# Two graph attention layers on one core: the scheduler's ring is booked in order of issue with nine slots, the seam's factors take a scalar operand, entry 1's mask moves to ScalarE, and strips run in longer blocks

## The chip, the cores and the metric

The kernel runs on one core of one Trainium2 chip. The metric is the device time of one execution in microseconds. Engines are named as in the profile: PE is TensorE's matmuls, PEld its weight loads, DVE is VectorE, ACT is ScalarE, POOL is GpSimd, SP is SyncE, which here issues the DMAs.

## The reference, cut to what matters

There are eight entries of 2048 nodes with 256 channels, and one adjacency matrix for all. Each entry goes through two layers, each followed by a residual sum and a layer norm.

```
# layer 0: eight heads of 32 channels
x_proj = einsum('bnd,hdf->bhnf', x, W)
e = leaky_relu(e_src[..., :, None] + e_dst[..., None, :], 0.2)
e = e + softplus(beta_tilde) * log(adj + 1e-6)
attn = softmax(where(adj > 0, e, -big))
x = layernorm(x + (attn @ x_proj, heads side by side) @ W_out.T)
# layer 1: one head of 256 channels
e = leaky_relu((x @ W1) @ (x @ W2).T, 0.2)
attention = softmax(where(adj > 0, e, -1e12))
x = layernorm(x + relu(attention @ (x @ W3)))
```

All values are float32.

## The kernel before

**Layer 0** takes two heads at a time (`HP = 2`, four pairs) and half of the rows (`rh`, 1024 of them). That is a unit, and there are eight units per entry. A unit has 16 tiles `s` of 128 partitions x 2 heads x 1024, one for each 128 columns of the adjacency (`jt`). A "strip" is PE's work on such a tile: `val` (the tile times the projected features) and, for some tiles, `den` (the tile times the denominators' weights), eight matmul instructions of 32 columns each, four side by side. From entry 2 on, tiles 11 to 15 of a unit are "direct": DVE makes the two heads' halves from the loaded mask `mt` (line 926), and PE adds up their denominators. Tiles 0 to 10 are "chain" tiles: ACT scales `mt` into the tile (line 399), DVE multiplies (line 926), and POOL adds the tile to the running `sums` (line 934), which PE takes in a last `close` strip. At a unit's end its heads are copied out (`evicted`), divided, and for the second pair of four heads multiplied on POOL (line 491).

**Layer 1** goes over 16 blocks of 128 rows per entry. For each, PE makes the scores `e` (line 1140), ACT copies them into one wide tile `p` (line 1146), DVE takes the mask `pen` off and finds the maximum (line 1185), POOL negates it (line 1186), ACT takes the exponential (line 1191), PE transposes `p` (`T`, line 1214), ACT copies that (line 1219), and PE multiplies with the values (`acc`, line 1233). ACT and DVE then finish the row block: `relu`, `z` (line 1255, which frees the PSUM bank of `acc`), statistics, norm, store.

**The seam** stands between an entry's two layers. PE multiplies the heads by `W_out` (`y`, line 1031), DVE adds the input (line 1035), takes statistics (line 1045), ACT makes the inverse deviation (lines 1051 and 1052), DVE the factor mean times inverse deviation (line 1057), ACT applies both (line 1064), and PE transposes (`tr`, line 1076) and makes the values (`h`, line 1090). Four groups of four row blocks pass through this.

**Order of the work.** Layer 0 of the first entry and the projections of all entries are in an order written out by hand. From then on a small scheduler in the kernel's Python (`Sched`) lays out all engines' instructions, each engine's in a fixed order: it keeps a clock for each engine and each task's assumed time (`busy`) and sets, step by step, the task that can start first. Layer 0 of the next entry (strips) is laid between layer 1 and the seam of the present one ("full" work). In what follows, entry 1 of the scheduled part means layer 1 of the first entry with layer 0 of the second beside it. Buffers are modelled by `Slots`, one list per ring; `Hold` is one use of a buffer that ends with its last reader. The actual buffer is handed out by the tile framework when the kernel is built, from a ring of nine with the tag "s" (`ring_tile`), which is used by the strips' tiles, by the wide tile `p` for all of an entry's layer 1, and by the second `ht` (the upper four heads), which later holds the seam's results.

PE chooses in `choose_pe` between the next full task and the next strip. The lag is the goal (strips in proportion to full work done, plus a lead) less the strips eaten. In a block of strips PE goes on while the lag is over `LOW`; from full work it turns to strips when the lag is over `HIGH` at an easy place and over `STRICT` within an iteration. It takes a strip as well when the full task isn't ready.

```
if f[0] > now + 0.35 or lag > (LOW if self.kind == "strip" else HIGH if easy else STRICT):
    return v[0], v[1], 0
return f[0], "full", f[1]
...
S.goal = lambda w: NP * 2 * NT * (w + 33.0) / span
```

In entry 1 the adjacency rows come in as integers, and the mask `pen` is made from them in two halves, the first on ACT (line 1168) and the second on DVE (line 1171); it is stored, and later entries load it.

Of the kernel before, what the change touches and what calls it, by code (L numbers as in the profile page):

```python
# [18 lines left out]
P = 128  # L19
# [8 lines left out]
def kernel(  # L28
# [38 lines left out]

    J2 = NT // 2
    DIRECT = [[range(NT)] * NP] + [[(11, 12, 13, 14, 15)] * NP] * (B - 1)
    SLOTS = 7  # L70

    const = ctx.enter_context(tc.tile_pool(name="const", bufs=1))
    dram = ctx.enter_context(tc.tile_pool(name="dram", bufs=1, space=DRAM))
# [19 lines left out]
    def ring_tile(name, shape=(P, N)):  # L93


        return wide.tile(list(shape), F32, tag="s", name=name, bufs=9)
# [414 lines left out]
    TURN = {False: 0.0, True: 0.14, ("T", "acc"): 0.11, ("acc", "T"): 0.05, ("acc", "e"): 0.08, ("e", "acc"): 0.085, ("T", "e"): 0.04,  # L511
            ("e", "T"): 0.03, ("e", "val"): 0.12, ("T", "val"): 0.13, ("acc", "val"): 0.08, ("val", "e"): 0.19, ("tr", "h3"): 0.1}
    WINDOW = 8
    LOW, HIGH, STRICT = -1.0, 1.5, 4.0
    NOW = [0.0]
    BACK = 2

# [6 lines left out]
    class Slots:  # L524
# [4 lines left out]
            self.free = [(0.0, tags[i] if tags else i) for i in range(n)]  # L529

        def at(self, n=0):
            return sorted(self.free)[n][0] if len(self.free) > n else None

        def take(self):
            got = min(self.free)
            self.free.remove(got)
            return got[1]

        def give(self, end, tag):
            self.free.append((end, tag))  # L540
# [21 lines left out]
    class Only:  # L562
# [8 lines left out]
        def take(self):  # L571
            self.slots.free.remove(next(f for f in self.slots.free if f[1] == self.tag))
            return self.tag

        def give(self, end, tag):
            self.slots.give(end, tag)
# [222 lines left out]
    S = Sched()  # L799
    bank = Banks(["m0", "m1", "den"])  # L800
    ring, mts, pts_s, hts, rows_s = (Slots(n, None, name) for n, name in ((SLOTS, "ring"), (4, "mt"), (4, "pts"), (4, "ht"), (4, "rows")))
    v_s, c_s, pen_s, xs_s = (Slots(n, None, name) for n, name in ((2, "v"), (0, "c"), (1, "pen"), (2, "xs")))

    def pe(where, name, busy, emit, deps=(), hold=None, reader=None, easy=True, seam=False):
# [50 lines left out]
    def unit(b, hp, rh, vs, vhold):  # L855
# [28 lines left out]
        prev_add = {}  # L884
        for jt in range(NT):
            chain = jt in u.chain
            slot = Hold(ring, 0)
            mt = Hold(mts, 2)
            ring_next = {"slot": slot}

# [3 lines left out]
            mload = S.add("mt", 0.35, load, takes=[mt], late=4.0)  # L894

            def begin(jt=jt):
                u.s[jt] = ring_tile("s", (P, HP, HALF))

            readers = 1 if jt in u.direct else 0
# [77 lines left out]
        if hp == 0 and rh == 0:  # L977
            hold = Hold(hts, 1)
            E.first_hold = hold
            u.evicted = S.add("evict", 0.5, u.copy_values, [u.vals[NT - 1]], takes=[hold])  # L980
        else:
            n = 4 if hp == 0 else 2
            deps = [u.vals[NT - 1]]
            frees = []
            if hp == 0:
                frees = [E.first_hold]
                deps.append(entries[b - 1].last_tr)
            if hp == HP and rh == 0:
                deps.append(entries[b - 1].last_tr)
            u.evicted = S.add("evict", 0.55 * n, u.copy_values, deps, frees=frees)  # L990
        dn = Hold(hts, 1)

        def dn_copy():
# [11 lines left out]
    def seam(b):  # L1005
# [9 lines left out]
        for g in range(NB):  # L1015
            xh, xn = Hold(hts, 2), Hold(xs_s, 2)

            def load(g=g):
                gat.xs[g] = chunk.tile([P, IG, D], F32, tag="ht", name="xg", bufs=4)
                nc.sync.dma_start(gat.xs[g], x[b].rearrange("(t p) d -> p t d", p=P)[:, ts(g, IG), :])  # L1020
            xl = S.add("x", 0.4, load, [E.start] if b else [], takes=[xh, xn], late=4.5)
            ys, st = [], {}
            deps = [E.mult[0, g // 2], E.mult[1, g // 2]]
            if old:
                deps.append(old.lastT)

            def y(t, k, g=g):
                yt = t.rearrange("p (t c) -> p t c", t=2)
                for i in range(2):
                    for kc in range(KC):  # L1030
                        nc.tensor.matmul(yt[:, i, :], gat.ht[kc][:, ts(g * IG + 2 * k + i, P)], wot[:, kc, :],  # L1031
                                         start=(kc == 0), stop=(kc == KC - 1))
            for k in range(2):
                def add(t, k=k, g=g):
                    nc.vector.tensor_add(gat.x1(2 * g + k), t.rearrange("p (t c) -> p t c", t=2), gat.xs[g][:, ts(k, 2), :])
                ys.append(pe("full", "y", 1.83, lambda t, k=k, y=y: y(t, k), deps, Hold(bank, 1), ("sum", 0.62, add, [xl]), seam=True))
            for k in range(2):
                ys[k].reader.deps += ys
                ys[k].reader.frees += [xh, xn]
            stats = []  # L1040
            for k in range(2):
                def stat(k=k, g=g):
                    if k == 0:
                        state["st", g] = small.tile([P, IG // 2, nc.vector.BN_STATS_DIM], F32, name="st4", bufs=2)
                    nc.vector.bn_stats(state["st", g][:, k, :], gat.x1(2 * g + k).rearrange("p t c -> p c t"))
                stats.append(S.add("stats", 0.65, stat, [ys[k].reader]))

            def lnexp(g=g):
                state["mv", g] = mv = state["st", g].rearrange("p a (t c) -> p (a t) c", t=2)
                state["f", g] = f = small.tile([P, 2, IG], F32, name="f4", bufs=2)  # L1050
                nc.scalar.activation(f[:, 0, :], mv[:, :, 2], AF.Ln, bias=eps_ln, scale=1.0 / D)
                nc.scalar.activation(f[:, 0, :], f[:, 0, :], AF.Exp, scale=-0.5)
            ln = S.add("ends", 0.52, lnexp, stats)

            def factor(g=g):
                f, mv = state["f", g], state["mv", g]
                nc.vector.scalar_tensor_tensor(f[:, 1, :], mv[:, :, 1], -1.0, f[:, 0, :], ALU.mult, ALU.mult)  # L1057
            fac = S.add("tinys", 0.1, factor, [ln])
            for k in range(2):
                def end(k=k, g=g):  # L1060
                    z, f = gat.x1(2 * g + k), state["f", g]
                    for i in range(2):
                        row = z[:, i, :]
                        nc.scalar.activation(row, row, AF.Identity, bias=f[:, 1, 2 * k + i:2 * k + i + 1],
                                             scale=f[:, 0, 2 * k + i:2 * k + i + 1])
                r = S.add("ends", 1.05, end, [fac])
                x1_ready[2 * g + k] = r

                def store(k=k, g=g):
                    nc.sync.dma_start(x1_d[b].rearrange("(t p) d -> p t d", p=P)[:, ts(2 * g + k, 2), :], gat.x1(2 * g + k))  # L1070
                E.done[2 * g + k] = S.add("out", 0.4, store, [r], late=3.0)
        for j in range(NT // 2):
            def tr(t, j=j):
                for kc in range(KC):
# [6 lines left out]
                nc.scalar.copy(gat.x1t[:, :, ts(j, 2 * P)], t.rearrange("p (k i) -> p k i", k=KC))  # L1081
            deps = [x1_ready[j], old.lastT if old else None]
            t = pe("full", "tr", 0.46, tr, deps, Hold(bank, 1), ("copy", 0.5, x1c, [old.lastE] if old else []), seam=True)
            trs.append(t)
            E.x1c[j] = t.reader

# [16 lines left out]
    def layer1(b):  # L1103
# [25 lines left out]
            h1[g] = (box, hold, out)  # L1129

        pbox = {}

        def scores(it, c):
            g = it // IG
            box, hold, qs = h1[g]
            r = R[it]

            def mm(t):
                for kc in range(KC):
                    nc.tensor.matmul(t, box["h"][:, kc, ts(it % IG, P)], gat.x1t[:, kc, ts(c, BK)],  # L1140
                                     start=(kc == 0), stop=(kc == KC - 1))

            def pre(t):
                if it == 0 and c == 0:
                    pbox["p"] = ring_tile("p")
                nc.scalar.activation(pbox["p"][:, ts(c, BK)], t, AF.Prelu, alpha=ALPHA)  # L1146
            deps = [qs[0].reader, qs[1].reader, E.x1c[2 * c], E.x1c[2 * c + 1]]
            if it == 0 and b > 0:
                deps.append(entries[b - 1].lastT)
            t = pe("full", "e", 1.74, mm, deps, Hold(bank, 1), ("copy", 0.5, pre, [R[it - 1]["T"][c]] if it else []), easy=(it == 0), seam=(it == 0))  # L1150
            t.frees = [hold]
            r["e"].append(t)

        def soft(it):
# [3 lines left out]
            if b == 0:  # L1158
# [5 lines left out]
                eh = [Hold(hts, 1), Hold(hts, 1)]  # L1164
                ld = S.add("row", 0.8, load, takes=[pen_hold] + eh, late=5.0)

                def half0():
                    nc.scalar.activation(r["pen"][:, ts(0, HALF)], r["edges"][0], AF.Relu, bias=no_edge, scale=-NO_EDGE)

                def half1():  # L1170
                    nc.vector.tensor_scalar(r["pen"][:, ts(1, HALF)], r["edges"][1], 0.0, NO_EDGE, ALU.is_le, ALU.mult)
                m0 = S.add("norm", 1.05, half0, [ld], frees=[eh[0]])
                m1 = S.add("stats", 1.15, half1, [ld], frees=[eh[1]], lock=True)
                S.add("out", 0.4, lambda: nc.sync.dma_start(pen_d[ts(it, P), :], r["pen"]), [m0, m1], late=3.0)
                pen = [m0, m1]
            else:
                def load():
                    r["pen"] = wide_tile("pen", "pen", 1, BF16)
# [28 lines left out]
        def turn(it, c):  # L1207
# [11 lines left out]
                nc.scalar.copy(pt, t)  # L1219
            t = pe("full", "T", 0.46, tr, [r["exp"]], Hold(bank, 1), ("copy", 0.5, cp, []), easy=(c < 1))  # L1220
            t.reader.takes = [hold]
            r["T"].append(t)

        def acc(it, h):
# [90 lines left out]
    for a in range(HP):  # L1315
        u.makes[NT - 1, a].after = lambda a=a: bank.give(u.makes[NT - 1, a].end, f"c{a}")
    span = 303.0
    S.goal = lambda w: NP * 2 * NT * (w + 33.0) / span
    S.run()
# [1 line left out]
_INS = ['x', 'adj', 'L0_gnn_W', 'L0_gnn_a_src', 'L0_gnn_a_dst', 'L0_gnn_beta_tilde', 'L0_gnn_W_out',  # L1321
# [27 lines left out]
```

## Time and profile before

| | |
|---|---|
| time, median of 3 runs | 4218.2 us (4212.86 to 4220.96) |
| the profiled execution | 4212.3 us, span 4210.1 us |
| PE, DVE, ACT, POOL busy | 4016.7, 3190.9, 2914.5, 2746.0 us |
| mean granted TensorE clock | 0.987 |
| DMA | 843.63 MB, mean 200 GB/s |

A busy share is an average over stages. PE's time counts a matmul from its start to a modelled end, and matmuls overlap, so PE's idle time is read from starts. In rows by line the columns are: line, engine, operation, tile written and tiles read, shapes, count, then busy us and mean ns, then the engine's idle time before them and what ended it. In rows of one tile the three numbers behind the count are the shortest, median and longest duration in ns. In a timeline they are start and length in us, then engine and line, and in brackets the idle time before and its releaser.

### The profile page before, as it was taken

The numbers are of one execution on the slowest core, as the hardware profiler recorded it, in microseconds if no ns is written. First come the engines' busy times: TensorE is split into PE (matmuls) and PEld (weight loads), VectorE is DVE, ScalarE is ACT, GpSimd is POOL, SyncE is SP. The second block draws the span as 40 slices with busy tenths as digits, with TensorE's granted clock in tenths as the row PEclk, the third lists the DMA queues.
The fourth block names the chain that finished last, engine by engine and source line by source line (L and its number), as shares of the span: only waits on it lengthen the run. The fifth ranks groups of instructions, "written<-read, shape, count | busy, mean of one in ns | idle before, by whom it ended". The sixth has DMA issues, their size and how long they took to land.

```text
span 4210.1 us, 60355 instructions
## 1 busy us (share of the span) xinstructions
PE 4016.7 (95%) x22704; PEld 2151.3 (51%) x22704; DVE 3190.9 (76%) x3263; ACT 2914.5 (69%) x4148; POOL 2746.0 (65%) x1318
## 2 busy tenths in 40 slices
PE   7899799998999999999999999999999999999999
PEld 5444344444555554454555545555555555555666
DVE  7888688877888888777888878787888887775222
ACT  6522467776787778776777778777777777776554
POOL 0000278877788886877878878888788886885000
PEclk9999899999999999999999999999999999999999
DMA  7888767666566666555666565656665665554111
GB/s 263 281 279 291 246 215 241 227 218 218 190 215 203 203 196 208 202 197 194 204 203 196 199 215 201 206 188 213 210 205 197 201 229 195 193 189 136 62 47 41
DMA packets 346437, 843.63 MB, mean 200 GB/s; under 512 B 49696, under 2 KB 166432, under 8 KB 346144
## 3 DMA queue, kind: packets, MB, share of 16 engines
q1 hardware_dynamic: 346144, 839.77, 59.6%
q8 instruction: 178, 2.92, 0.3%
q14 instruction: 115, 0.94, 0.1%
HBM read 763.76 MB, written 75.37 MB: 199 GB/s over the span
## 4 chain that ended last, share of the span: by engine, by line
PE 63%; ACT 8%; DVE 7%; POOL 5%; DMA 3%; issue 3%; SPq 0%; DVEq 0%; ACTq 0%; POOLq 0%
PE e L1140 19%; PE acc L1233 17%; PE val L445 13%; POOL sums L934 5%; PE den L445 4%; DVE s L926 4%; PE T L1214 4%; ACT s L399 4%; PE h L1090 3%; PE h L1116 2%; ACT p L1146 1%; DMA mt<-mt_d 1%; DVE f L1057 1%; DVE p L1185 1%; PE y L1031 1%
## 5 line engine op out<-in xcount | busy, mean ns | idle before, releaser
L934 POOL TENSOR_TENSOR sums<-sums,s 128x1024 f32<-128x1024 f32 x1008 | 2365.7, 2385 | 29.3 <-DVE s L926 27.3
L926 DVE SCALAR_TENSOR_TENSOR s<-c,re,s 128x1024 f32<-128x1024 f32 x1232 | 1512.9, 1274 | 304.6 <-ACT s L399 252.2
L399 ACT ACTIVATE s<-mt,re 128x1024 f32<-128x1024 f32 x1232 | 1353.9, 1146 | 127.5 <-DMA mt<-mt_d 58.8
L445 PE MATMUL val<-s,v 128*32 128x512 f32 x8192 | 1026.1, 599 | 41.4 <-DVE s L413 13.7
L1140 PE MATMUL e<-x1t,h 128*128 128x512 f32 x2048 | 988.9, 607 | 45.4 <-ACT p L1146 33.7
L1233 PE MATMUL acc<-h,pts 128*128 128x256 f32 x4096 | 927.5, 382 | 0.7 <-ACT pts L1219 0.7
L1233 PEld LDWEIGHTS acc<-h,pts 128*128 128x128 f32 x4096 | 768.4, 190 | 226.5 <-issue 106.2
L926 DVE SCALAR_TENSOR_TENSOR s<-c,re,mt 128x1024 f32<-128x1024 f32 x560 | 682.5, 1274 | 93.0 <-POOL sums L934 86.6
L1140 PEld LDWEIGHTS e<-x1t,h 128*128 128x128 f32 x2048 | 352.9, 191 | 402.0 <-issue 269.9
L445 PEld LDWEIGHTS val<-s,v 128*32 128x32 f32 x8192 | 236.2, 109 | 608.2 <-issue 478.0
L1185 DVE CUSTOM_DVE_ANT_0 p<-p,pen 128x2048 f32<-128x2048 f32 x128 | 320.2, 2502 | 229.8 <-ACT p L1146 228.7
L1146 ACT ACTIVATE p<-e 128x512 f32<-128x512 f32 x512 | 304.3, 594 | 202.5 <-PE e L1140 198.0
L445 PE MATMUL den<-s,re 128*32 128x512 f32 x3264 | 438.7, 593 | 0.0
L1186 POOL TENSOR_SCALAR neg<-neg 128x1 f32<-128x1 f32 x128 | 26.7, 208 | 627.8 <-DVE neg L1185 627.8
L934 POOL TENSOR_TENSOR sums<-s 128x1024 f32<-128x1024 f32 x112 | 266.9, 2402 | 254.3 <-DVE s L926 218.3
L1191 ACT ACTIVATE p<-p,neg 128x2048 f32<-128x2048 f32 x128 | 256.1, 2001 | 246.6 <-POOL neg L1186 246.3
L1214 PEld LDWEIGHTS T<-ident,p 128*128 128x128 f32 x2048 | 251.0, 141 | 275.5 <-issue 174.6
L413 DVE SCALAR_TENSOR_TENSOR s<-c_in,re,mt 128x1024 f32<-128x1024 f32 x256 | 310.4, 1277 | 49.1 <-DMA mt<-mt_d 36.7
L1214 PE MATMUL T<-ident,p 128*128 128x128 f32 x2048 | 309.8, 275 | 21.7 <-ACT p L1191 19.1
L1219 ACT COPY pts<-T 128x512 f32<-128x512 f32 x512 | 297.0, 583 | 28.0 <-PE T L1214 27.2
L286 POOL PARTITION_ALL_REDUCE top<-top x8 | 6.6, 820 | 431.0 <-DVE top L285 415.1
L445 PEld LDWEIGHTS den<-s,re 128*32 128x32 f32 x3264 | 109.3, 110 | 243.3 <-issue 240.7
(100 smaller groups left out, 2538.1 us busy)
## 6 DMA issues: line engine op xcount, KB each, us to landing
mt<-mt_d SPq DMA_DIRECT2D x992, 512.0 KB
c_in<-c_d SPq DMA_DIRECT2D x64, 1024.0 KB
pen<-pen_d SPq DMA_DIRECT2D x112, 512.0 KB
xg<-in_x_dram SPq DMA_DIRECT2D x60, 512.0 KB
adj_t<-in_adj_dram SPq DMA_DIRECT2D x16, 1024.0 KB
mt_d<-mt SPq DMA_DIRECT2D x32, 512.0 KB
rb<-rec_d SPq DMA_DIRECT2D x128, 128.0 KB
adj_r<-in_adj_dram SPq DMA_DIRECT2D x32, 512.0 KB
```

Of the source, the lines that this page charges most:

```text
L399: nc.scalar.activation(self.s[jt][:, a], self.mt[jt], AF.Copy, scale=self.gat.re[:, 1, jt, h:h + 1])
L413: nc.vector.scalar_tensor_tensor(s[:, a], self.c[a], self.gat.re[:, 0, jt, h:h + 1], m, ALU.max, ALU.mult)
L445: nc.tensor.matmul(dst[ts(q, DH), :], weights[q % 2], s[:, q % 2, ts(q // 2, BK)], start=start, stop=stop)
L926: nc.vector.scalar_tensor_tensor(u.s[jt][:, a], u.c[a], gat.re[:, 0, jt, h:h + 1], m, ALU.max, ALU.mult)
L934: nc.gpsimd.tensor_tensor(u.sums[:, a], of[:, a], u.s[jt][:, a], ALU.add)
L1140: nc.tensor.matmul(t, box["h"][:, kc, ts(it % IG, P)], gat.x1t[:, kc, ts(c, BK)], start=(kc == 0), stop=(kc == KC - 1))
L1146: nc.scalar.activation(pbox["p"][:, ts(c, BK)], t, AF.Prelu, alpha=ALPHA)
L1185: nc.vector.tensor_tensor_reduce(p, p, r["pen"], 1.0, -FMAX, ALU.subtract, ALU.max, neg)
L1191: nc.scalar.activation(p, p, AF.Exp, bias=r["neg"], accum_out=den)
L1214: nc.tensor.transpose(t[:, ts(k, P)], pbox["p"][:, ts(c * IG + k, P)], ident)
L1219: nc.scalar.copy(pt, t)
L1233: nc.tensor.matmul(r["acc"], r["pts"][g][:, ts(k, P)], gat.h3[:, j, :], start=(j == 0), stop=(j == NT - 1))
```

## The change

It has five parts.

1. `Slots` gives out the buffer that was given back first in order of issue, where it was the one with the earliest free time. This holds for all rings.
2. The ring is booked with nine slots instead of seven. What was left out before (the wide tile `p` and the second `ht`) is now booked by `Hold`s of its own: one per entry for `p`, from the first score copy to the last transpose, and one for the heads, from the copy to the seam's stores and transposes. The class `Spare` lets strips' tiles take a slot only if enough are left for these two (`keep` counts how many are reserved).
3. The seam's factor is made by four `tensor_scalar` instructions over one element each instead of one `scalar_tensor_tensor` over four, and is booked with 0.35 instead of 0.1 us.
4. In entry 1 both halves of the mask are made on ACT.
5. `LOW`, `HIGH` and `STRICT` are -2, 4 and 8 instead of -1, 1.5 and 4; the lead is 28 instead of 33.

```
-    SLOTS = 7
+    SLOTS = 9
...
-    LOW, HIGH, STRICT = -1.0, 1.5, 4.0
+    LOW, HIGH, STRICT = -2.0, 4.0, 8.0
...
         def at(self, n=0):
-            return sorted(self.free)[n][0] if len(self.free) > n else None
+            return self.free[n][0] if len(self.free) > n else None
 
         def take(self):
-            got = min(self.free)
-            self.free.remove(got)
-            return got[1]
+            return self.free.pop(0)[1]
...
+    class Spare:
+        def __init__(self, slots):
+            self.slots, self.keep, self.name = slots, 0, "spare"
+
+        def at(self, n=0):
+            return None if self.slots.at(n + self.keep) is None else self.slots.at(n)
+
+        def take(self):
+            return self.slots.take()
 
         def give(self, end, tag):
             self.slots.give(end, tag)
...
+    spare = Spare(ring)
+    spare.keep = 1
+    heads_hold = [Hold(ring, 2 * NB + NT // 2)]
+    heads_hold[0].take()
...
-            slot = Hold(ring, 0)
+            slot = Hold(spare, 0)
...
             def begin(jt=jt):
+                if jt == 0 and hp == HP and rh == 0:
+                    spare.keep += 1
                 u.s[jt] = ring_tile("s", (P, HP, HALF))
...
-            u.evicted = S.add("evict", 0.55 * n, u.copy_values, deps, frees=frees)
+            takes = []
+            if hp == HP and rh == 0:
+                heads_hold.append(Hold(ring, 2 * NB + NT // 2))
+                takes = heads_hold[-1:]
+
+            def copy():
+                if takes:
+                    spare.keep -= 1
+                u.copy_values()
+            u.evicted = S.add("evict", 0.55 * n, copy, deps, takes=takes, frees=frees)
...
+                if b and g == 0 and k == 0:
+                    spare.keep += 1
...
-                nc.vector.scalar_tensor_tensor(f[:, 1, :], mv[:, :, 1], -1.0, f[:, 0, :], ALU.mult, ALU.mult)
-            fac = S.add("tinys", 0.1, factor, [ln])
+                for i in range(IG):
+                    nc.vector.tensor_scalar(f[:, 1, i:i + 1], mv[:, i, 1:2], f[:, 0, i:i + 1], -1.0, ALU.mult, ALU.mult)
+            fac = S.add("tinys", 0.35, factor, [ln])
...
+        E.p_hold = Hold(ring, NT * NB)
...
                 if it == 0 and c == 0:
                     pbox["p"] = ring_tile("p")
+                    spare.keep -= 1
...
-                def half0():
-                    nc.scalar.activation(r["pen"][:, ts(0, HALF)], r["edges"][0], AF.Relu, bias=no_edge, scale=-NO_EDGE)
-
-                def half1():
-                    nc.vector.tensor_scalar(r["pen"][:, ts(1, HALF)], r["edges"][1], 0.0, NO_EDGE, ALU.is_le, ALU.mult)
-                m0 = S.add("norm", 1.05, half0, [ld], frees=[eh[0]])
-                m1 = S.add("stats", 1.15, half1, [ld], frees=[eh[1]], lock=True)
-                S.add("out", 0.4, lambda: nc.sync.dma_start(pen_d[ts(it, P), :], r["pen"]), [m0, m1], late=3.0)
-                pen = [m0, m1]
+                made = []
+                for k in range(2):
+                    def half(k=k):
+                        nc.scalar.activation(r["pen"][:, ts(k, HALF)], r["edges"][k], AF.Relu, bias=no_edge, scale=-NO_EDGE)
+                    made.append(S.add("norm", 1.05, half, [ld], frees=[eh[k]]))
+                S.add("out", 0.4, lambda: nc.sync.dma_start(pen_d[ts(it, P), :], r["pen"]), made, late=3.0)
+                pen = made
...
-    S.goal = lambda w: NP * 2 * NT * (w + 33.0) / span
+    S.goal = lambda w: NP * 2 * NT * (w + 28.0) / span
```

Left out above are the lines that end the new `Hold`s: the seam's `y`, its stores and transposes give back the heads' slot, and each `T` gives back a part of `p`'s.

More of the change, by code (lines that the diff above doesn't have):

```diff
@@ L573, in take, with give @@
             return self.tag
+        def give(self, end, tag):
+            self.slots.give(end, tag)
+    class Spare:
[5 more added lines that the diff above has]
+            return self.slots.take()
         def give(self, end, tag):
@@ L1023, in seam @@
             deps = [E.mult[0, g // 2], E.mult[1, g // 2]]
+            held = heads_hold[-1]
             if old:
@@ L1036, in seam @@
                 ys.append(pe("full", "y", 1.83, lambda t, k=k, y=y: y(t, k), deps, Hold(bank, 1), ("sum", 0.62, add, [xl]), seam=True))
+                ys[k].frees = [held]
             for k in range(2):
@@ L1070, in store @@
                     nc.sync.dma_start(x1_d[b].rearrange("(t p) d -> p t d", p=P)[:, ts(2 * g + k, 2), :], gat.x1(2 * g + k))
-                E.done[2 * g + k] = S.add("out", 0.4, store, [r], late=3.0)
+                E.done[2 * g + k] = S.add("out", 0.4, store, [r], frees=[held] if k else [], late=3.0)
         for j in range(NT // 2):
@@ L1083, in seam @@
             t = pe("full", "tr", 0.46, tr, deps, Hold(bank, 1), ("copy", 0.5, x1c, [old.lastE] if old else []), seam=True)
+            if j % 2:
+                t.frees = [held]
             trs.append(t)
@@ L1151, in scores @@
             t.frees = [hold]
+            if it == 0 and c == 0:
+                t.reader.takes = [E.p_hold]
             r["e"].append(t)
@@ L1221, in turn @@
             t.reader.takes = [hold]
+            t.frees = [E.p_hold]
             r["T"].append(t)
```

## The prediction

> **What bounds the kernel now.** I read the page first, then the windows of the nine entries of the work, the chain in order of time, and the three places where a line of the change stands in the trace.
>
> The page, whose columns are busy time, share of the span and instructions:
>
> ```profile
> span 4210.1 us, 60355 instructions
> ...
> PE 4016.7 (95%) x22704; PEld 2151.3 (51%) x22704; DVE 3190.9 (76%) x3263; ACT 2914.5 (69%) x4148; POOL 2746.0 (65%) x1318
> ...
> PE 63%; ACT 8%; DVE 7%; POOL 5%; DMA 3%; issue 3%; SPq 0%; DVEq 0%; ACTq 0%; POOLq 0%
> ```
>
> TensorE carries 63% of the chain. What can be won is the time in which it waits, and what it loses at changes of kind. The windows (length, then busy time of PE, PEld, DVE, ACT, POOL, then clock, DMA share, GB/s) are cut where the y matmuls of each seam begin:
>
> ```profile
> 0.00:511.00 511.00, 444.44 (x3153) 227.10 (x3153) 394.06 (x353) 206.77 (x325) 17.37 (x20) 0.96 0.82 273
> 511.00:1050.00 539.00, 501.44 (x2729) 249.32 (x2730) 446.48 (x436) 398.65 (x535) 435.15 (x202) 0.98 0.67 224
> 1050.00:1523.00 473.00, 460.91 (x2594) 246.01 (x2593) 387.23 (x396) 360.98 (x502) 391.11 (x184) 0.99 0.61 204
> ...
> 2970.00:3441.00 471.00, 464.16 (x2627) 244.76 (x2625) 390.99 (x404) 366.89 (x509) 389.19 (x184) 1.00 0.62 207
> ...
> 3903.00:4210.00 307.00, 295.72 (x1217) 205.33 (x1215) 70.26 (x136) 155.05 (x293) 3.32 (x16) 0.98 0.15 51
> ```
>
> The first 511 us are written out by hand and the change does not reach them. The last 307 us are layer 1 of the last entry alone, with no strip beside it. Only the 3392 us between can move: 539 us for entry 1 and 462 to 492 us for each of the six behind it. Entry 1 is some 60 us longer than the others, with more busy time on DVE (446 against 387).
>
> In that stretch and the tail I went through the matmuls' starts and took out each matmul's own pace (0.43 us for four parallel strip matmuls or one `e`, 0.215 for an `acc`, 0.109 for a transpose). Gaps over 0.45 us sum to 131 us: 43 in entry 1, 13, 25, 19, 8, 6 and 10 in the next six, 6 in the last. By what ended them: 36 us `DVE ht L1035` in the seams, 26 us `ACT p L1146`, 23 us `ACT p L1191`, 14 us `DVE z L1255`. Besides, there are 311 blocks of strips (64 in entry 1, 38 to 44 in each other).
>
> **The change part by part.**
>
> *Factors of the seam.* One `scalar_tensor_tensor` over 4 elements becomes four `tensor_scalar` over one. The rows (shortest, median, longest ns):
>
> ```profile
> L1264 DVE TENSOR_SCALAR f<-f x128: 153/154/156, 633.0 to 4205.8; 128x1 f32<-128x1 f32 x128
> ...
> L1057 DVE SCALAR_TENSOR_TENSOR f<-st,f x32: 141/1410/6683, 519.3 to 3921.5; 128x4 f32<-128x4 f32 x32
> ```
>
> The old one needs 0.14 us and took 1.634 in the mean: it is held while the sums on POOL run. The four beside the last seam, where POOL has nothing, took 0.16 each. The Trainium skill (SBUF — State Buffer, "Who interferes with whom") says why: an instruction with two SBUF inputs contends with a GpSimd instruction that reads SBUF. The same section speaks against the replacement: `tensor_scalar` can enter a 2-port mode, which contends as well. By that rule four instructions might each be held, 4 x 1.4 us = 5.6 us, worse than now. The row of L1264 decides: 128 one-element `tensor_scalar` with POOL busy around most of them, none over 156 ns. So four cost 0.62 us, and each factor is shorter by 1.0 us on average, 32 us of DVE in all (the unheld ones lose 0.46 each, inside that mean). How much is on the path? Take the seam at 1535:
>
> ```profile
> 1535.03 3.72 PE L1031 MATMUL y<-wot,ht 128*128 128x256 f32 x16 [1.14 <-DVE ht L1035]
> 1538.68 1.06 PE L445 MATMUL den<-sums,ones 128*32 128x512 f32 x8
> 1539.56 1.90 PE L445 MATMUL val<-s,v 128*32 128x512 f32 x16
> 1546.42 2.93 PE L1031 MATMUL y<-wot,ht 128*128 128x256 f32 x6 [4.96 <-DVE ht L1035]
> ```
>
> A factor held for 6.68 us (1537.9 to 1544.5) stands in DVE's queue before the `sum` that frees the bank, and PE idles 5 us. Eight such gaps follow a factor held over 2 us (1.7, 3.5, 5.0, 5.4, 1.9, 2.7, 0.9, 4.5 = 25.6 us); capped by what each factor loses beyond 0.62, 22 us. The sum or the scale before it will be late next in some: I take 16, ends 8 and 32.
>
> *Ring in order of issue, nine slots.* The kernel's ring has nine buffers; the planner booked seven and took the one that it thought free earliest. The trace shows that this isn't the buffer handed out:
>
> ```profile
> 898.45 0.16 DVE L1197 RECIPROCAL rec<-den 128x1 f32<-128x1 f32 x1 [2.46 <-ACT p L1191]
> 907.97 2.48 DVE L926 SCALAR_TENSOR_TENSOR s<-c,re,mt 128x1024 f32<-128x1024 f32 x2 [9.35 <-POOL sums L934]
> ...
> 913.77 0.41 DVE L1255 TENSOR_TENSOR z<-acc,x1r 128x256 f32<-128x256 f32 x1
> ```
>
> A direct tile, which itself needs nothing of POOL, waits 9.35 us for a sum there: it got a buffer that a sum still reads. Behind it is queued `z`, which frees the bank that the next PE group needs, and PE stands for 6.2 us until 914.2. The waits list has 90.6 us of DVE and 42.5 us of ACT (`s L399`) behind POOL in this way. Gaps of PE right behind them: 3.2, 6.4, 3.8, 2.3, 3.3 in entry 1; 3.3, 3.3, 2.9, 1.3, 4.7 later; 34.5 us. With the right buffer booked, the planner can set `z`, the mask and the copies ahead of such a tile; the tile itself still waits. Extra room adds little, since the buffers exist already. The true order of the ring isn't shown beyond these waits, and a new plan makes new collisions: lower end a loss of 8, upper a gain of 34; I take 14, under half, as the sums themselves are no sooner done.
>
> *Longer blocks of strips.* A block ended at one strip ahead of the goal and began at 1.5 behind (4 within an iteration); now 2 ahead, 4 and 8 behind. The cost of a change of kind, from the chain in order of time:
>
> ```profile
> 1146.56 4.43 PE val L445 x40
> ...
> 1213.45 5.29 PE val L445 x48
> ```
>
> Eight more are 0.86 us, so forty are 4.30, and leaving the block costs 0.13. Entering it, from the same starts, 0.12 behind an `acc` and 0.09 behind a `T`. The rule of the skill (TensorE: Matmul & The Clock Gate, "Step-by-step: what each phase is for"), that weight loads are pulled ahead of running matmuls, would make a change of kind free and this part worth 0; the trace has 114 exits to `acc` with a median of 0.129. A block saved is worth 0.25, less what its neighbours then lose to each other (`acc` to `T` 0.11, `T` to `e` nothing): 0.2. Blocks are now 3 tiles of 128 per entry; from 4 behind to 2 ahead is 6, so at least 21 per entry. Blocks will be cut where tiles aren't ready: I take 30 per entry, 210 for 311, 101 x 0.2 = 20 us. Ends: 0 and 162 x 0.25 = 40.
>
> *Entry 1's mask.* `pen` line L1171 leaves DVE: 16 x 1788 ns = 28.6 us; its shortest is 693, so 17.5 us are waits for POOL. ACT gets 16 more of L1168 (1143 ns), 18.3 us, behind the same loads. In the fullest stretches of entry 1 (680 to 800) DVE is busy 52 to 53 of 60 us, POOL 50 to 53, ACT 46 to 47: ACT covers it with about 1 us per mask. But POOL is next, so of DVE's 28.6 us I count 2% of 340 us, 6 us; ends 17 gained, and 4 lost if ACT's copies come late. No DMA is added, and SP's order there changes only by the plan.
>
> *Lead 33 to 28, reservations.* Strips come later by 5 us of full work, 5 x 477/303 = 8 us, and some 0.75 strips (3 us) by the thresholds' mean. What hides it: the last multiply of the heads on POOL ends 37, 18, 23, 18, 24, 22 and 10 us before the first y of the seven seams behind. Only the last is reached. I take 2 us lost, ends 0 and 15. The bookings are Python and cost no instruction.
>
> Sum: -16 - 14 - 20 - 6 + 2 = -54 us. The profiled execution took 4212.3 us (span 4210.1), so it would be 4158; the median of the runs, 4218.2, lies 5.9 above it, which gives 4164.
>
> **The rivals.**
> A, only the local repairs pay (factors, mask, and a few us of turns, since blocks are cut by tiles not ready): 16 + 6 + 8, 4188. For it: 43 us of PE's gaps lie in one entry, so the other six are already close to full.
> B, the plan comes out better all round (factors 25, ring 30, turns 35, mask 10): 4118. Against it: all PE gaps behind 511 us are only 131.
> C, slower: longer gaps between blocks keep tiles in the ring until POOL has none to add. A tile is scaled and made in about 5 us and then waits for PE up to 14 us (6 strips of 2.37 us of full work), 19 in all, at one tile per 3.7 us: 5.1 buffers. With 8 behind it is 24 us, 6.5. Seven or eight are there. It turns bad once the wait passes 7 x 3.7 - 5 = 21 us. Then POOL idles, which has 10 us to spare per unit of 16 tiles and 60 us (busy 395 of 478 in the eight units between 2492 and 2970); each us beyond that costs 1 us in each of 56 units, and with the repairs' 30 won, 1.5 us beyond gives 4218 - 30 + 84 = 4272. Against it: all POOL waits before the sums are 284 us now, mostly for tiles not made.
> D, the booking does nothing, since the sums are the true limit: 4164 + 14 = 4178, inside the first case's range.
>
> **How the numbers follow.** First case with D 0.60 (4140 to 4182), A 0.20, B 0.10, C 0.10. 0.2%, about 8 us, is what a measurement of this kernel can tell from no change. A's lower part and a mild C make the middle: faster 0.87, same 0.05, slower 0.08. The range from B's to A's weak end, 4115 to 4205, leaves out C and little else.
>
> **What would show it.** Right: L1057 at about 155 ns x128; 200 to 230 strip blocks; DVE behind POOL in `s<-c,re,mt` well under 90 us; entry 1 shorter by over 20 us; POOL's busy time unchanged. Wrong: L1057 held again, POOL's idle before the sums above 350 us, y waiting for `POOL ht L491`, or as many blocks as before.

## The result and the profile after

The changed kernel takes 4175.15 us (median of 4 runs, 4174.46 to 4180.99); before, on the same chip, 4215.76. The ratio is 0.9905, interval 0.9888 to 0.9923, so some 40 us are won, where 54 were forecast. Below, a difference of 0.001 in a ratio to before is 4.2 us; versions are compared by their ratios, as each was timed against before on its own chip.

The page of after, busy time, share and instructions:

```profile
span 4173.0 us, 60538 instructions
...
PE 3986.3 (96%) x22704; PEld 2159.0 (52%) x22704; DVE 3149.2 (75%) x3343; ACT 2929.8 (70%) x4164; POOL 2748.0 (66%) x1318
```

POOL has the same work, DVE 42 us less. Lines have moved: in the views of the changed kernel 945, 953, 1066, 1090, 1183, 1228 and 1293 are the lines 926, 934, 1035, 1057, 1146, 1191 and 1255 of before. The chain of waits breaks off in this profile after 9% of the span, so I read the windows instead, cut at the seams as before (length, then PE, PEld, DVE, ACT, POOL busy, clock, DMA share, GB/s):

```profile
0.00:513.00 513.00, 445.48 (x3153) 225.64 (x3153) 393.68 (x353) 206.92 (x325) 17.18 (x20) 0.96 0.83 272
513.00:1015.00 502.00, 481.93 (x2679) 246.72 (x2680) 412.38 (x430) 409.11 (x545) 427.41 (x199) 0.99 0.73 237
1015.00:1484.00 469.00, 458.99 (x2620) 245.99 (x2619) 379.39 (x404) 359.30 (x501) 382.69 (x182) 1.00 0.63 204
...
2927.00:3402.00 475.00, 461.23 (x2624) 246.54 (x2623) 381.69 (x408) 365.02 (x505) 385.93 (x183) 0.99 0.62 204
...
3865.00:4173.00 308.00, 296.64 (x1217) 205.94 (x1215) 71.65 (x148) 155.24 (x293) 3.34 (x16) 0.98 0.16 50
```

Nearly all of the gain lies in entry 1 (539 to 502 us). The six entries behind it take 2850 us together; before it was 2853. Yet their factor is no longer held, and there are 68 fewer blocks of strips in them.

To see where that went I counted the lost time between PE's starts again, from the first seam to the last, now with four strip matmuls side by side as one. The starts are sorted by size: 0.04 to 0.15 us (changes of kind, and small steps within full work), 0.15 to 0.45, and over 0.45 (waits).

| | 0.04 to 0.15 us | 0.15 to 0.45 | over 0.45 | all, with the rest |
|---|---|---|---|---|
| before | 106.9 us, 1073 | 53.8 | 110.0 | 279.1 |
| after | 81.7 us, 836 | 46.4 | 106.2 | 242.1 |
| after with the old block limits (`u_limits`) | 108.7 us, 1091 | 23.9 | 44.8 | 188.4 |

The difference of the first two, 37.0 us, is close to the 40 us by which this stretch became shorter (3392 to 3352). The first column fell by 25 us. Some 16 of these lie at changes between strips and full work, which is 0.2 us for each of the 78 blocks saved; the rest lies mostly between two full matmuls. But PE waits almost as long as before, although three causes of waiting were repaired. A new wait must stand there, and the last row says where it comes from.

### The profile page after: what moved, and what is told of

The parts are those of the page before. It is cut to its first block, busy times and chain, and to the rows that moved or that the text cites. A ratio compares the mean times of both kernels' runs of the same rounds, so it can differ in the third digit from the quotient of the medians.

```text
span 4173.0 us, 60538 instructions
## 1 busy us (share of the span) xinstructions
PE 3986.3 (96%) x22704; PEld 2159.0 (52%) x22704; DVE 3149.2 (75%) x3343; ACT 2929.8 (70%) x4164; POOL 2748.0 (66%) x1318
## 5 line engine op out<-in xcount | busy, mean ns | idle before, releaser
L399 ACT ACTIVATE s<-mt,re 128x1024 f32<-128x1024 f32 x1232 | 1350.3, 1146 | 136.9 <-DMA mt<-mt_d 63.4
L1271 PE MATMUL acc<-h,pts 128*128 128x256 f32 x4096 | 912.4, 380 | 0.8 <-ACT pts L1256 0.8
L445 PEld LDWEIGHTS val<-s,v 128*32 128x32 f32 x8192 | 245.3, 110 | 627.2 <-issue 488.2
L1222 DVE CUSTOM_DVE_ANT_0 p<-p,pen 128x2048 f32<-128x2048 f32 x128 | 340.0, 2656 | 269.5 <-ACT p L1183 262.0
```

The lines of the kernel that those rows point to most:

```text
L399: nc.scalar.activation(self.s[jt][:, a], self.mt[jt], AF.Copy, scale=self.gat.re[:, 1, jt, h:h + 1])
L445: nc.tensor.matmul(dst[ts(q, DH), :], weights[q % 2], s[:, q % 2, ts(q // 2, BK)], start=start, stop=stop)
L1222: nc.vector.tensor_tensor_reduce(p, p, r["pen"], 1.0, -FMAX, ALU.subtract, ALU.max, neg)
L1271: nc.tensor.matmul(r["acc"], r["pts"][g][:, ts(k, P)], gat.h3[:, j, :], start=(j == 0), stop=(j == NT - 1))
```

## The experiments

All are the changed kernel or the kernel before with parts exchanged. "Limits" are `LOW`, `HIGH`, `STRICT`.

| version | median us | ratio to before | interval |
|---|---|---|---|
| changed kernel | 4175.2 | 0.9905 | 0.9888 to 0.9923 |
| ... old limits and lead 33 | 4153.0 | 0.9856 | 0.9843 to 0.9868 |
| ... half of the mask on DVE | 4200.5 | 0.9971 | 0.9958 to 0.9983 |
| ... factor as one instruction | 4196.6 | 0.9957 | 0.9943 to 0.9970 |
| ... without the ring's booking | 4162.6 | 0.9883 | 0.9867 to 0.9899 |
| ... lead 33, new limits | 4170.9 | 0.9900 | 0.9885 to 0.9915 |
| ... old limits, lead 28 | 4112.0 | 0.9767 | 0.9755 to 0.9780 |
| ... old limits, lead 23 | 4123.1 | 0.9786 | 0.9770 to 0.9801 |
| ... LOW -2, HIGH and STRICT old | 4135.9 | 0.9816 | 0.9800 to 0.9833 |
| ... LOW -1, HIGH and STRICT new | 4128.8 | 0.9803 | 0.9789 to 0.9818 |
| before, factor alone | 4184.7 | 0.9936 | 0.9922 to 0.9950 |
| before, factor and mask | 4145.7 | 0.9848 | 0.9835 to 0.9861 |
| before, factor, mask, lead 28 | 4122.6 | 0.9787 | 0.9773 to 0.9801 |

### The parts undone, one at a time

```
u_blocks:  -LOW, HIGH, STRICT = -2.0, 4.0, 8.0   +-1.0, 1.5, 4.0
           -(w + 28.0)                           +(w + 33.0)
```

> The changed kernel with the old block rules alone (LOW, HIGH, STRICT -1, 1.5, 4 and the lead of 33). Theory T, that the gain of fewer changes of kind (311 to 233 blocks, 0.2 us each, 15 us) is given back by longer waits that the blocks themselves bring (strips later, banks and ring slots held longer): 4170 to 4182 us, blocks back at 290 to 320, PE's gaps over 0.45 us behind the hand-written part some 15 us fewer than the changed kernel's 138. Rival R, that the blocks are worth what I put on them and the ring's booking gives it back: 4190 to 4200 us, gaps as many as in the changed kernel.

Measured: 0.9856. It is 21 us faster than the changed kernel, where even theory T had forecast no more than a draw. There are 333 blocks instead of 233. The seven later entries' lengths show a split: entry 1 is 23 us longer (525), the six others 45 us shorter (2805). So R is out: the blocks' package costs, it doesn't earn.

```
u_mask:    m0 on ACT, m1 = S.add("stats", 1.15, half1, [ld], frees=[eh[1]], lock=True) on DVE, as before
```

> The changed kernel with the second half of entry 1's mask back on DVE. Theory M, that most of the 37 us by which entry 1 became shorter come from DVE's relief: entry 1 (513 to 1015) longer by 15 to 28 us, the whole 4190 to 4203 us. Rival, that the ring's booking is what shortened it and the mask is worth the 6 us of the prediction: 4178 to 4184 us. The other entries should not move by more than 5 us in sum in either.

Measured: 0.9971, 28 us slower, as theory M said; entry 1 went to 526 us. The row of the half on DVE (shortest, median, longest ns):

```profile
L1210 DVE TENSOR_SCALAR pen<-adj_r x16: 947/1949/7886, 540.1 to 1006.1; 128x1024 bf16<-128x1024 int32 x16
```

It is held up to 7.9 us. The six later entries are 8 us longer in sum, where 5 were allowed for. But the execution that was profiled is the slowest of its eight, 10 us over their median, so these 8 us can't be put down to the version.

```
u_factor:  -for i in range(IG): nc.vector.tensor_scalar(f[:, 1, i:i + 1], mv[:, i, 1:2], f[:, 0, i:i + 1], -1.0, ...)
           +nc.vector.scalar_tensor_tensor(f[:, 1, :], mv[:, :, 1], -1.0, f[:, 0, :], ALU.mult, ALU.mult)   # booked 0.1
```

> The changed kernel with the one two-input instruction for the seam's factor, booked with 0.1 us as it was. If the factor's share is what the prediction said, 4188 to 4195 us, with the factor held up to 6 us again in some seams and PE gaps behind DVE in the seams up from 14 to over 30 us. If the sum behind it is late anyway, 4173 to 4179 us.

Measured: 0.9957, 22 us slower. The held instruction is back:

```profile
L1089 DVE SCALAR_TENSOR_TENSOR f<-st,f x32: 147/978/6841, 520.1 to 3909.2; 128x4 f32<-128x4 f32 x32
```

PE's gaps over 0.45 us in the seams behind `DVE ht` rose from 12 to 27 us, so 15 of the 22 us stand there. The 22 us are more than the 16 of the prediction, and the median lies 2 us above the range given here.

```
u_ring:    the kernel before with the factor, the mask, LOW, HIGH, STRICT = -2.0, 4.0, 8.0 and lead 28
```

> The changed kernel with seven slots and the earliest-free rule, without the bookings for the wide tile and the heads. If the booking is worth what the prediction said, 4185 to 4195 us, with DVE's waits behind POOL in front of direct tiles back at 80 us or more and PE gaps behind z. Rival R (the booking gives back what the blocks gain): 4155 to 4168 us. A third view, that the longer blocks need the slots: over 4200 us, since seven booked slots cut the blocks and strips fall behind.

Measured: 0.9883, 9 us faster than the changed kernel, but the two intervals overlap. The time falls into rival R's range, but not for R's reason, since `u_blocks` shows that the blocks gain nothing that could be given back. DVE in front of direct tiles waits 58 us behind POOL and ACT in front of chain tiles 49, together 107. With the booking it is 41 and 59, together 100: with these limits the booking moves waits from DVE to ACT and removes hardly any.

### One part alone, and the blocks' package divided

```
a_factor:  the kernel before with four tensor_scalar, still booked 0.1
```

> The kernel before with the factor as four one-element instructions, its booking left at 0.1 us, so that every engine's order of instructions is that of before. Theory: the held instruction itself costs what the prediction put on it, 16 us: 4195 to 4202 us, PE's gaps behind DVE ht in the seams down from 36 to about 15. Rival: in the changed kernel the factor was worth its 21 us through the new plan, and by itself less than 8: 4207 us or more.

Measured: 0.9936, 27 us faster, more than forecast. The order of all engines is that of before, so this is the instruction itself, and of all parts it is the one that is cleanly isolated. Its row:

```profile
L1058 DVE TENSOR_SCALAR f<-st,f x128: 191/204/218, 517.4 to 3885.0; 128x1 f32<-128x1 f32 x128
```

PE's gaps over 0.45 us in the seams fell from 41 to 18 us, those behind `DVE ht` from 34 to 14. The profiled execution, the fastest of its six, is 37 us shorter than that of before; up to 12 of the other 14 us (an estimate) go with the clock, whose stretches at half speed fell from 55 to 31 us (last section).

```
a_two:     the kernel before with the factor (booked 0.35) and both halves of the mask on ACT
```

> The kernel before with the factor and the mask alone. If the two are worth what taking them out of the changed kernel cost (21 and 25 us) and add up: 4166 to 4174 us, as fast as the whole change, so that booking and blocks together are worth nothing. If the mask is worth that only with the new blocks in entry 1: 4180 to 4192 us.

Measured: 0.9848, 64 us faster, far more than either expectation. Two parts of the change alone beat the whole by 24 us. The window of entry 1 in the version with the factor alone:

```profile
509.00:1043.00 534.00, 498.23 (x2732) 247.90 (x2730) 438.87 (x449) 398.98 (x535) 433.95 (x202) 0.98 0.68 226
```

and in this one:

```profile
509.00:1020.00 511.00, 493.18 (x2744) 246.45 (x2744) 419.68 (x439) 415.82 (x552) 435.92 (x204) 0.99 0.73 238
```

DVE (third busy time) has 19 us less, ACT 17 more, POOL 2 more, and the entry is 23 us shorter. PE's gaps over 0.45 us in it fell from 34 to 20 us, and those behind `DVE z` from 14 us to none. The version also books the factor with 0.35 us, so the 37 us between the two are mask, booking of the factor and new order together.

```
u_lead:    the changed kernel, (w + 33.0)
u_limits:  the changed kernel, LOW, HIGH, STRICT = -1.0, 1.5, 4.0
```

> The changed kernel with the lead back at 33 and the new limits of the blocks. If it is the lateness of the strips that makes ACT wait at the seams for slots that POOL's sums still hold: 4150 to 4160 us, as with both undone. If it is the size of the blocks: 4170 to 4180 us.

> The changed kernel with LOW, HIGH, STRICT back at -1, 1.5, 4 and the new lead of 28. If the size of the blocks is what costs: 4150 to 4160 us, some 45 us won in the six later entries and some 20 lost in entry 1. If the lead is: 4170 to 4180 us.

Measured: 0.9900 and 0.9767. The first is as the size of the blocks would have it; the second is 38 us below the lower of its two ranges. With the new limits the lead makes no difference that the intervals resolve. With the old limits and the new lead the kernel takes 4112 us, 58 us less than the changed kernel and 98 less than before; it is the fastest of all versions, and faster than both kernels. The new limits cost 58 us at a lead of 28 and 19 us at 33 (0.9856 against 0.9900). The old limits were expected to lose 20 us in entry 1; it came out at 507 us, only 5 longer. The other six are 2787 us, 62 shorter.

The waits lists show what differs (who waited for whom: us, times, longest). The changed kernel:

```profile
ACT s L399 <- POOL sums L953: 59.0, 23, 10.4
DVE s L945 <- POOL sums L953: 40.8, 18, 10.0
```

With the old limits:

```profile
DVE s L945 <- POOL sums L953: 31.2, 16, 4.7
...
ACT s L399 <- POOL sums L953: 23.0, 17, 4.3
```

54 us instead of 100, and none over 5 us. One of the long ones in the changed kernel, on PE, ACT and DVE in turn:

```profile
1839.61 5.36 PE L445 MATMUL val<-s,v 128*32 128x512 f32 x48
...
1848.44 1.88 PE L1151 MATMUL h<-x1t,w 128*128 128x512 f32 x4
1858.33 2.07 PE L1151 MATMUL h<-x1t,w 128*128 128x512 f32 x2 [8.00 <-DVE z L1293]
```

```profile
1840.75 2.19 ACT L399 ACTIVATE s<-mt,re 128x1024 f32<-128x1024 f32 x2 [0.56 <-PE val L445]
1852.06 1.15 ACT L399 ACTIVATE s<-mt,re 128x1024 f32<-128x1024 f32 x1 [9.12 <-POOL sums L953]
1853.11 0.43 ACT L1287 ACTIVATE acc<-acc,rec 128x256 f32<-128x256 f32 x1
```

```profile
1856.66 1.28 DVE L945 SCALAR_TENSOR_TENSOR s<-c,re,mt 128x1024 f32<-128x1024 f32 x1 [6.74 <-POOL sums L953]
1857.86 0.41 DVE L1293 TENSOR_TENSOR z<-acc,x1r 128x256 f32<-128x256 f32 x1
```

PE has just eaten the strips of seven tiles in one block (1839.6 to 1847.5). ACT wants a slot for the next tile, and the slot comes free only when POOL has summed; it waits 9.12 us. Behind it in ACT's fixed order stands the `relu` of the finished `acc`, behind that `z` on DVE, which itself stands behind a direct tile's wait of 6.74 us; and `z` frees the bank that the next PE group needs. PE stands for 8 us; the wait that ends last is that of the direct tile on DVE. That the long block is what put POOL so far behind is argued from this order of events; no run shows it by itself. The loss doesn't end there, since the clock is at half from 1852.7 to 1862.9 us, and PE's first 4.6 us of work behind the wait run at half speed:

```profile
1852.80:1862.90 10.10, 4.58 (x10) 2.07 (x10) 4.76 (x7) 5.26 (x10) 3.82 (x2) 0.50 0.30 90
```

From the first seam to the last, the trace has 55 us at half clock in the changed kernel, as many in the kernel before, and 17 with the old limits. PE loses at most half of such time, so by estimate up to 19 of the 58 us are lost through the clock and not in the waits themselves. At the seams the same is seen in front of `y`: 12.5 us of gaps behind `z` in the changed kernel, none with the old limits.

### The best version's parts

```
v_noring:  the kernel before with the factor, the mask and (w + 28.0)
v_end:     the changed kernel, LOW, HIGH, STRICT = -2.0, 1.5, 4.0
v_start:   the changed kernel, LOW, HIGH, STRICT = -1.0, 4.0, 8.0
v_lead23:  the changed kernel, LOW, HIGH, STRICT = -1.0, 1.5, 4.0 and (w + 23.0)
```

> The kernel before with the factor, the mask and the lead of 28: the best version so far without the ring's booking. If the booking is worth nothing by itself and the lead brought the 41 us from the version with lead 33: 4105 to 4120 us. If the lead pays only because the booking then fits the room that is really there: 4135 to 4150 us, DVE and ACT together behind POOL for slots over 85 us instead of 54.

Measured: 0.9787. It lies between the two expectations. The lead brings 26 us without the booking and 37 with it; the booking at a lead of 28 brings 8 us, with intervals that overlap. DVE and ACT wait 89 us behind POOL for slots, with the booking 54. So here the booking goes with two fifths fewer of these waits, but 35 us less waiting of two engines came with 8 us of time, and even these are not resolved.

> The changed kernel with HIGH and STRICT back at 1.5 and 4 and LOW kept at -2: blocks begin as early as before and go on for one strip more. If it is the late start of the blocks (strips up to 4 or 8 behind the goal, with made tiles waiting in the ring) that costs the 63 us: 4110 to 4125 us. If it is their going on: 4150 to 4175 us.

> The changed kernel with LOW back at -1 and HIGH and STRICT kept at 4 and 8: blocks begin late and end as before. If the late start costs: 4150 to 4175 us, and DVE's and ACT's waits behind POOL for slots at 90 us or more, as in all versions with the new limits. If the going on costs: 4110 to 4125 us and waits near 54.

Measured: 0.9816 and 0.9803, both between the ranges given. Going on for longer costs 21 us, starting later 15 us, both together 58. Neither one alone is the cause. `v_start` contradicts what I expected of it: its waits behind POOL for slots are only 28 us, the fewest of these versions, and yet PE's waits over 0.15 us are 89 us, where the old limits have 69. Slot waits are therefore one of the ways in which long blocks cost, seen at 1840, and not all of it; the rest isn't shown.

> The changed kernel with the old limits and a lead of 23. If later strips go on paying as from 33 to 28 (41 us with the old limits): 4085 to 4105 us. If the slack of the heads' last multiply before the seam's y (10 to 18 us) is then used up: 4115 to 4140 us, with gaps of PE in front of y behind POOL ht. If the 41 us were partly the luck of one plan: anything from 4110 to 4150 us without such gaps.

Measured: 0.9786. There is no further gain, the interval overlaps that of lead 28, and no `y` waits for `POOL ht`, which is the third view (the luck of one plan); PE's waits over 0.15 us are 66 us, as many as at 28 (69). Between 33 and 28 they fell from 100 to 69 us. Why strips that start later make PE wait less is left open: the waits behind POOL for slots are 55 and 54 us, so it isn't these.

## Why the prediction was right or wrong

The time fell into the range, and the direction was right, but that the sum came out is luck, as two errors cancel: the repairs were worth more than I put on them, and the blocks, which I had as the largest gain, are a loss. From the versions, one part after the other: factor 27, mask 37, lead 26, booking 8, limits -58, in all 40 us. The signs that the prediction named for being right came true or nearly so (233 blocks, entry 1 shorter by 37 us, DVE's waits at 41 us, POOL's busy time unchanged, the factor at 203 ns), but none of them tests whether fewer blocks save time.

- **Factor, 16 forecast, 22 to 27 measured.** The mechanism is right, the size too small: 1.4 to 1.7 times as much was won. I capped each gap of PE in the seam by what the factor loses and then took 16 of 22, and the sum had no term for the clock, which in the trace of before is at half for 6.8 us at the gap of 4.96 us too (from 1544.2). The four instructions take 0.20 us each, not 0.155; of 128 none was held (191 to 227 ns in the changed kernel). So the row of L1264 pointed the right way on whether such instructions are held; their length it did not give.
- **Ring, 14 forecast, -9 to 8 measured.** With all else equal, the booking took DVE's waits behind POOL in front of direct tiles from 58 to 41 us, but ACT's rose from 49 to 59 (`u_ring` against the changed kernel). What failed is the step that takes 14 of the 34.5 us of PE's gaps behind such waits as won: the new order has waits of its own, as the one at 1840.
- **Blocks, 20 forecast with ends 0 and 40; 58 lost.** The step's own arithmetic held: 0.2 us for each block, though 78 were saved and not 101. What failed is its lower end. I wrote 0, as if nothing could be lost, and kept the loss for rival C, with POOL running out of tiles. POOL doesn't: its idle time before a unit's first sum fell from 254 to 217 us. With the old limits PE's waits over 0.15 us are 69 us, with the new 153: 84 more, for 27 saved in the steps below 0.15. Of the 84, up to 19 are the clock's (estimate above).
- **Mask, 6 forecast, 28 to 37 measured.** The step "POOL is next, so of DVE's 28.6 us I count 2%" failed. I compared busy shares of stretches in which no engine was full. Entry 1 became 23 us shorter with POOL's busy time unchanged (434 and 436), so POOL was not the next bound. What the shares don't show are single places where DVE's fixed order is in PE's way: PE's gaps behind `DVE z` in this entry went from 14 us to none. How much of that the mask's own time did, and how much the new order, isn't separated.
- **Lead, 2 lost forecast; 26 to 37 won with the old limits, nothing resolved with the new.** I had looked only for what later strips could delay. The seams' slack did cover it, as I had said; where the gain comes from is open.

Rival C's mechanism is refuted by POOL's idle time; its direction, that longer blocks can cost more than their changes of kind save, was right. Of the booking, D (it does nothing) is what the runs come nearest to. What stays open is how much of each part depends on the single order that the planner happens to lay: but for `a_factor`, which keeps the order of before, every version is one new order, and no version was run with the order alone disturbed.

## What to carry to other kernels

Before crediting a saving at switches, ask who lives off the short blocks: in a kernel whose engines have fixed orders, one slot wait holds everything queued behind it. Here longer blocks saved 27 us of small steps and brought 84 us of waits, of which such slot waits are a part. Look for small instructions that are far longer than their work and stand in front of something that frees a bank; replacing those by ones that were never held here was worth 27 us for one line. A change of several parts that comes out near its forecast is not understood until the parts have been run apart: this one hides a version of 4112 us.

## What the runs showed of the hardware that I had not expected

A one-element `tensor_scalar` with a scalar read from SBUF and a second multiplication takes 0.203 us in the median, one with a single constant 0.154 (which of the two differences costs the 0.05 us isn't shown). None of either was held, though POOL's sums run beside most of them:

```profile
L1090 DVE TENSOR_SCALAR f<-st,f x128: 191/203/227, 521.4 to 3885.2; 128x1 f32<-128x1 f32 x128
...
L1302 DVE TENSOR_SCALAR f<-f x128: 153/154/156, 624.9 to 4168.7; 128x1 f32<-128x1 f32 x128
```

A wait of PE can cost more than its length. After one of 3.83 us in the changed kernel the first groups of eight strip matmuls, 0.86 us each elsewhere, start 1.13, 1.70 and 1.46 us apart:

```profile
3363.61 0.66 PE L1251 MATMUL T<-ident,p 128*128 128x128 f32 x4 [3.83 <-ACT p L1228]
3364.20 1.38 PE L445 MATMUL val<-s,v 128*32 128x512 f32 x8
3365.33 1.95 PE L445 MATMUL den<-s,re 128*32 128x512 f32 x8
3367.03 1.64 PE L445 MATMUL val<-s,v 128*32 128x512 f32 x8
3368.49 1.04 PE L445 MATMUL den<-s,re 128*32 128x512 f32 x8
```

The windows around it have the granted clock behind POOL's busy time, 1.00 and then 0.72:

```profile
3358.00:3364.00 6.00, 2.17 (x13) 1.62 (x11) 6.00 (x8) 5.88 (x7) 2.44 (x2) 1.00 1.04 287
3364.00:3370.00 6.00, 6.00 (x43) 1.61 (x45) 5.90 (x11) 3.94 (x5) 6.00 (x4) 0.72 0.98 341
```

The four groups took 5.15 us (3364.20 to 3369.35) where four times 0.86 are 3.44, so 1.7 us were lost beside the wait itself.

From the first seam to the last, the changed kernel's trace has 11 stretches at half clock, of 3.4, 6.8 or 10.2 us. Each goes with a wait of PE: six with the waits of 3.83 us and more, five with waits of 2.02 to 2.74 us, of which this is the shortest, with the clock behind it:

```profile
3309.37 0.66 PE L1251 MATMUL T<-ident,p 128*128 128x128 f32 x4 [2.02 <-ACT p L1228]
```

```profile
3310.30:3313.60 3.30, 3.30 (x20) 0.87 (x16) 3.20 (x6) 3.17 (x5) 3.30 (x2) 0.50 0.46 158
```

Others of that length, 2.71 us at 962.7 and 2.57 at 2201.6, were not followed by one. The Trainium skill (TensorE: Matmul & The Clock Gate, "HAM oscillation — how this bites in real kernels") warns of gaps over about 3.4 us. The waits from 3.83 us on agree; those of 2 to 2.7 us show that here shorter ones can bring it too.
